# Sorting the neighbour lists of the first two blocks, and starting each layer on them beside the last tails of the layer before

## The chip, the cores and the metric

The kernel runs on one NeuronCore of a Trainium2 chip. The metric is the device time of one execution in microseconds, taken as the median of several runs; less is better. The engines are called PE (TensorE, matmuls), DVE (VectorE), ACT (ScalarE), POOL (GpSimd, which also issues every indirect transfer) and SP (SyncE).

## The reference

Four graph layers run over 2048 nodes, a batch of 8 and 128 features. All use one random adjacency matrix in which an entry is 1 with chance 1/128, so a node has about 16 neighbours. Layers 0 and 1 are attention layers with 8 heads, layers 2 and 3 are graph attention with one score per edge:

```
# layers 0 and 1
Q, K, V = h@Wq, h@Wk, h@Wv                          # 8 heads of 16
attn = softmax(where(adj == 0, -inf, Q.K / 4))       # over the neighbours m of n
x = layernorm(h + attn@V @ Wo + bo)
x = layernorm(x + relu(x@W1 + b1)@W2 + b2)
# layers 2 and 3
h = x@W;  e = leaky_relu(h@a_src [of i] + h@a_dst [of j], 0.2)
out = softmax(where(adj == 0, -inf, e)) @ h
x = layernorm(out + x)
```

## The kernel before, in words

**Places and blocks.** The kernel treats the matrix as sparse. `start()` reads it, lists the neighbours of every node, and counts the nodes by their number of neighbours. `rank` holds the place of each node in falling order of that number, and `perm` holds the nodes by place. The 2048 places are cut into 16 blocks of 128 nodes (t = 0 to 15), one node to a partition. Block t has `CAPS[t]` list slots, 30 for block 0 down to 11 for block 15. The last two slots of block 0 (`FOLD`) are a folded part that holds the further neighbours of the 16 largest nodes. A list that is shorter than its block's slots ends in entries that point outside the table. `find_lists(t)` fills `lists` and the mask `lmask` for one block; it runs beside layer 0.

**Tables.** Layer l reads its neighbours' rows from the DRAM tensor `tables[l]`: one row for each node, of 8 x 256 floats (keys and values, 8 KB) in layers 0 and 1, and of 8 x 130 floats (4160 bytes) in layers 2 and 3. `gather` (L299) is one indirect transfer, issued by POOL, that fetches the rows of one list slot for the 128 nodes of a block. Since neighbours are random, a slot can need any row of the table. `put_rows` (L419) is the indirect transfer that writes a finished block's rows into the table of the next layer.

**Chunks.** A layer's slots are worked off in chunks, of two slots in layers 0 and 1 and of four in layers 2 and 3. A chunk's rows land in one of six buffers (`KVB`), and up to three chunks (four in layers 2 and 3, `AHEAD`) are fetched ahead of the one in work. An attention chunk is a product on DVE (L528), a sum on DVE (L531), exponentials on ACT (L537), a product on DVE (L542) and matmuls with the identity that add the slots up in PSUM (L552). A chunk of layers 2 and 3 is four small DVE operations (L667 to L673), a large product on DVE (L679) with the last two of eight batches on ACT (L684), an addition of halves on DVE (L688), and matmuls (L694).

**Tails.** When a block's last chunk is done, `sums` takes reciprocals of the weights' sums, `outputs` (L565, L571) scales the accumulator, and two tails (`attention_tail` or `gat_tail`, one for each half of the batch) do the projections, the layer norms and the next layer's rows. A norm is squares on ACT (L406), a power on POOL (L411) and a scaling on ACT (L415). When both halves are done, `state_done` stores the block's state to DRAM (`kept`) and calls `put_rows`.

**Order.** The order of every engine's instructions is written by hand. Chunks and tails are Python generators; each `yield` ends a step. The main loop in `layer(l)` makes one trip for each chunk, in which it issues the chunk's own steps and calls `slot()` three times; a `slot()` advances every open tail by one step. At the end of a layer `drain()` runs the open tails to their ends, and only then does the next call of `layer` issue its first gathers. So the three boundaries between layers are places where the last tails run with no chunk beside them: the first gathers of layer l + 1 come after the last `put_rows` of layer l.

**Other names the change touches.** `w` holds a block's weights (one buffer), `val` a row of the matrix in `start()` (two buffers), `qf` the queries for the folded part of block 0, `over` collects the overflow checks that `verdict()` turns into a flag; if it is not zero, a general dense path follows.

Of the kernel before, what the change touches and what calls it, by code (L numbers as in the profile page):

```python
# [8 lines left out]
F32 = mybir.dt.float32  # L9
F16 = mybir.dt.float16  # L10
BF16 = mybir.dt.bfloat16
FP8 = mybir.dt.float8e4
I32 = mybir.dt.int32
# [4 lines left out]
P = 128  # L18
B, N, D = 8, 2048, 128
NT = N // P  # L20
NH = 8
# [7 lines left out]
NB = 8  # L29
CHUNK = 4 * NB * (D + 2)  # L30
KVB = 6
AHEAD = (3, 3, 4, 4)
SCALED = 2


# [1 line left out]

BASE, MANY, FOLD = 28, 16, 2
CAPS = [BASE + FOLD, 23, 21, 20, 19, 18, 18, 17, 16, 16, 15, 14, 14, 13, 12, 11]
SEG = 128  # L40
BINS = 64

# [4 lines left out]
def split(s, n):  # L47

    k = -(-s // n)
    return [s // k + (i < s % k) for i in range(k)]  # L50


def pieces(t, n):

    res, k = [], 0
    for m in split(CAPS[t] if t > 0 else BASE, n):
        res.append((k, m, False))
        k += m
    if t == 0:
        res.insert(1, (BASE, FOLD, True))  # L60
    return res


# [1 line left out]
def sparse_path(ctx: ExitStack, tc: tile.TileContext, ins: dict, out: bass.AP, flag: bass.AP):  # L65
# [60 lines left out]
    def buffer():  # L126
        turn[0] += 1
        return bufs[turn[0] % KVB]
# [4 lines left out]
    lists = const.tile([P, sum(CAPS)], I32, name="lists")  # L133
    lmask = const.tile([P, sum(CAPS)], F32, name="lmask")
    first = [sum(CAPS[:t]) for t in range(NT)]

    own = const.tile([P, NT, B], F32, name="own")
    score = const.tile([P, 2, NT, 2 * B], F32, name="score")
# [142 lines left out]
    def width(l):  # L281
        return NB * (2 * D if l < 2 else D + 2)
# [12 lines left out]
        nc.sync.dma_start(xT.rearrange("p b n -> p (b n)"), kept[t])  # L295
        return xT

    def gather(l, at, dst):
        nc.gpsimd.indirect_dma_start(  # L299
            out=dst, out_offset=None, in_=tables[l][:, :],  # L300
            in_offset=bass.IndirectOffsetOnAxis(ap=lists[:, at : at + 1], axis=0),
            bounds_check=N - (l < 2), oob_is_err=False,
        )

# [23 lines left out]
    def find_lists(t):  # L328
# [45 lines left out]
        )  # L374
        yield

    def folded_sums(w, box):

        columns = w.shape[-1]
        ps = misc()[:, :columns]  # L380
        for i in range(FOLD):
            nc.tensor.matmul(ps, merge, w[:, i, :], start=i == 0, stop=i == FOLD - 1)
        box["folded"] = small.tile([P, columns], F32, tag="folded", name="folded", bufs=1)
        nc.scalar.copy(box["folded"], ps)
# [15 lines left out]
    def normed(z, dst):  # L400

        yield

        ss = small.tile([P, 4], F32, tag="ss", name="ss", bufs=3)
        for i in range(4):
            nc.scalar.activation(  # L406
                dst[:, i, :], z[:, i, :], AF.Square, bias=eps, scale=D**-0.5,
                accum_out=ss[:, i : i + 1],
            )
        rs = small.tile([P, 4], F32, tag="rs", name="rs", bufs=3)  # L410
        nc.gpsimd.tensor_tensor(rs, ss, half, op=ALU.pow)  # L411
        yield
        yield
        for i in range(4):
            nc.scalar.mul(dst[:, i, :], z[:, i, :], rs[:, i : i + 1])  # L415
        yield

    def put_rows(l, t, rows):
        nc.gpsimd.indirect_dma_start(  # L419
# [54 lines left out]
    def state_done(l, t, box):  # L474


        box["halves"] = box.get("halves", 0) + 1
        if box["halves"] == 2:
            if l < 3:
                nc.sync.dma_start(kept[t], box["x"].rearrange("p b n -> p (b n)"))  # L480
                put_rows(l + 1, t, box["rows"])
            box["state"](t + 3)


    def attention_begin(l, t, box):
# [2 lines left out]
            yield  # L488
        xT = box["x"]
        if t == 0:  # L490
            qf = work.tile([P, NB, D], F32, tag="q", name="qf")
        box["q"] = q = work.tile([P, NB, D], F32, tag="q", name="q")
        for i in range(0, NB, 4):
            pq = misc().rearrange("p (b c) -> p b c", c=D)
# [25 lines left out]
    def attention_chunk(l, c):  # L520
        box, t, k, ns = c["box"], c["t"], c["k"], c["ns"]
        if k == 0:
            box["acc"] = pacc.tile([P, NB // 4, 512], F32, tag="acc", name="acc")
            box["w"] = work.tile([P, max(CAPS), NB * NH], F32, tag="w", name="w", bufs=1)
        acc, w, q = box["acc"], box["w"], box["qf" if c["folded"] else "q"]
        kv = c["buf"].rearrange("p s (b c) -> p s b c", b=NB)
        kk = kv[:, :, :, :D]
# [212 lines left out]
    def start():  # L740
# [81 lines left out]
            nc.scalar.activation(junk, src, AF.Relu, bias=onesc, scale=-1.0, accum_out=dst)  # L822

        def neighbours(t):
            val = work.tile([P, N], F16, tag="val", name="val")
            nc.vector.scalar_tensor_tensor(
                val, adj[t % 6], 0.0, iota1, op0=ALU.not_equal, op1=ALU.mult
            )
# [69 lines left out]
        part1 = small.tile([P, NT], F32, tag="part1", name="part1", bufs=1)  # L898
        nc.vector.tensor_copy(part1, pn[:, :NT])
        nc.vector.tensor_add(perm, part1, pn[:, NT : 2 * NT])  # L900

        nc.vector.scalar_tensor_tensor(
            over[:, 0, :], left, float(N - N // SEG * 8), none, op0=ALU.add, op1=ALU.subtract
# [31 lines left out]
    threads = []  # L935
    tails = []

    def advance(group):
        for g in list(group):
            if next(g, 0) == 0:  # L940
                group.remove(g)

    def slot():
        advance(threads)
        advance(tails)

    def drain():
        while threads or tails:
            advance(threads)
            advance(tails)  # L950

    def tail(l, t, box):
        def rest():
            for _ in range(2 if l < 2 else 3):
                yield
            outputs(l, t, box)
            part = attention_tail if l < 2 else gat_tail
            tails.append(part(l, t, box, 0))
            tails.append(later(3, lambda: part(l, t, box, 4)))
            yield  # L960

        tails.append(rest())

    def later(n, make):
        for _ in range(n):
            yield
        yield from make()

    def layer(l):
        boxes = [{} for _ in range(NT)]  # L970
        att = l < 2
        per = 2 if att else 4
        chunks = []
        for t in range(NT):
            for k, ns, folded in pieces(t, per):
                chunks.append(dict(t=t, k=k, ns=ns, folded=folded, box=boxes[t], last=False))
            chunks[-1]["last"] = True
        n = len(chunks)

        def fetch(c):  # L980
            if c >= n:
                return
            c = chunks[c]
            c["buf"] = buffer()[:, : c["ns"] * width(l)].rearrange("p (s c) -> p s c", s=c["ns"])
            for i in range(c["ns"]):
                gather(l, first[c["t"]] + c["k"] + i, c["buf"][:, i])

        def state(t):
            if t < NT:
                if l == 0:  # L990
                    threads.append(fetch_state(t, boxes[t]))
                else:
                    boxes[t].update(x=load_state(t), ready=True)

        for box in boxes:
            box["state"] = state

        def begin(t):
            if att:
                threads.append(attention_begin(l, t, boxes[t]))  # L1000

        if l == 0:
            threads.append(find_lists(0))
            state(0)
            drain()
        for i in range(AHEAD[l]):
            fetch(i)
        if l > 0:
            state(0)
        drain()  # L1010
        begin(0)
        drain()
        if l == 0:
            threads.append(find_lists(1))
        run = [(attention_chunk if att else gat_chunk)(l, c) for c in chunks]

        def go(i, times=1):

            if 0 <= i < n:
                for _ in range(times):  # L1020
                    next(run[i], None)

        def is_last(i):
            return 0 <= i < n and chunks[i]["last"]

        def end(i):
            t = chunks[i]["t"]
            tail(l, t, chunks[i]["box"])

        for i in range(n + 2):  # L1030
            fetch(i + AHEAD[l])
            if i < n and chunks[i]["k"] == 0:
                t = chunks[i]["t"]
                if l == 0 and t + 2 < NT:
                    threads.append(find_lists(t + 2))
                if t == 0:
                    state(1)
                    threads.append(later(12, lambda: state(2) or iter(())))
                while att and "asked" not in chunks[i]["box"]:
                    advance(threads)  # L1040
            if i + 2 < n and chunks[i + 2]["k"] == 0:
                begin(chunks[i + 2]["t"])
            if att:

                go(i - 2)
                if is_last(i - 2):
                    end(i - 2)
                go(i)
                slot()
                go(i)  # L1050
                slot()
                if is_last(i - 1):
                    sums(l, chunks[i - 1]["t"], chunks[i - 1]["box"])
                go(i - 1, 2)
                slot()
            else:


                if i + 1 < n and chunks[i + 1]["folded"]:
                    go(i + 1)  # L1060
                if is_last(i - 1):
                    sums(l, chunks[i - 1]["t"], chunks[i - 1]["box"])
                go(i)
                slot()
                go(i)
                slot()
                go(i - 1, 2)
                if is_last(i - 1):
                    end(i - 1)
                slot()  # L1070
        if l == 3:
            verdict()
        drain()

    with tc.manual_schedule():
        start()
        for l in range(4):
            layer(l)


@with_exitstack
# [522 lines left out]
```

## Time and profile before

| what | value |
|---|---|
| median of 3 runs | 3457.39 us (3457.35 to 3460.24) |
| the profiled execution | 3462.36 us, of which the span is 3460.6 us |
| busy share of the span | PE 79%, PE weight loads 46%, DVE 88%, ACT 41%, POOL 61% |
| mean granted PE clock | 0.916 |
| gathers (L299) | 1108, mean 1465 ns on POOL each |
| writes of rows (L419) | 48, mean 1537 ns on POOL each |
| DMA traffic | 980 MB, 283 GB/s over the span |
| DVE busy in layer 1, 1280 to 2240 us | 952.28 of 960 us |
| DVE busy in layer 2, 2340 to 2840 us | 430.58 of 500 us |

The busy shares are means over four layers and a preparation of some 180 us. The page also cuts the span into 40 slices of 86.5 us and gives each engine's busy share in tenths for each slice; stages with different limits are told apart there.

### The profile page before, as it was taken

What the parts mean: (1) busy time and instruction counts of PE and PEld (TensorE: products, weight loads), DVE (VectorE), ACT (ScalarE), POOL (GpSimd) and SP (SyncE); (2) the same over time, 40 slices, a digit from 0 to 9 for tenths busy, and PEclk for the clock granted to TensorE, in tenths of its full rate; (3) what the DMA queues carried; (4) which work ended last, traced back from release to release, by engine and by line L of the source; (5) the groups of instructions that cost most, each with busy time, mean ns of one, the idle gap of its engine ahead of it and who ended that gap; (6) DMA issues with size and microseconds to landing.
All of it is one profiled execution on the core that took longest, in us unless ns stands there. A gap on an engine that the chain in (4) does not pass through costs nothing. (4 is left out here: it accounts for less than half of the span.)

```text
span 3460.6 us, 34591 instructions
## 1 busy us (share of the span) xinstructions
PE 2749.7 (79%) x10618; PEld 1587.6 (46%) x10618; DVE 3055.0 (88%) x2685; ACT 1435.0 (41%) x4972; POOL 2125.4 (61%) x1441
## 2 busy tenths in 40 slices
PE   5657888799899966888888989975888995668675
PEld 4523455455555542444555556652444552223332
DVE  7789999999999929999999999938888875888886
ACT  5612333344344440233333434443555663444444
POOL 0053666666667533555677766628878756888874
PEclk9878999899999989989999999998999997988888
DMA  8486778888878547777887888729999967989883
GB/s 339 179 306 248 282 280 299 321 294 304 315 295 313 211 167 281 266 295 294 307 299 306 293 305 304 283 69 337 334 327 346 336 266 275 321 301 317 299 292 123
DMA packets 195887, 980.13 MB, mean 283 GB/s; under 512 B 28334, under 2 KB 30128, under 8 KB 124084
## 3 DMA queue, kind: packets, MB, share of 16 engines
q0 software_dynamic: 172352, 884.08, 70.2%
q1 hardware_dynamic: 18438, 75.51, 5.7%
q10 hardware_dynamic: 4904, 18.24, 1.4%
q8 instruction: 87, 1.43, 0.2%
q14 instruction: 106, 0.87, 0.1%
HBM read 937.13 MB, written 85.21 MB: 295 GB/s over the span
## 5 line engine op out<-in xcount | busy, mean ns | idle before, releaser
L299 POOL DMA_INDIRECT kv<-table,lists x1108 | 1622.8, 1465 | 523.7 <-issue 240.9
L552 PE MATMUL acc<-kv,ident 128*128 128x512 f32 x2200 | 1110.6, 636 | 257.7 <-DVE kv L542 257.4
L694 PE MATMUL acc<-kv,ident 128*128 128x512 f32 x1184 | 610.2, 664 | 236.7 <-DVE kv L688 191.1
L552 PEld LDWEIGHTS acc<-kv,ident 128*128 128x128 f32 x2200 | 413.4, 201 | 698.6 <-issue 368.2
L528 DVE TENSOR_TENSOR kv<-kv,q 128x2048 f32<-128x2048 f32 (+1 forms) x282 | 629.3, 2232 | 69.5 <-DMA kv<-table,lists 63.3
L531 DVE TENSOR_REDUCE sc<-kv 128x128 f32<-128x2048 f32 (+1 forms) x284 | 634.1, 2233 | 9.4
L411 POOL TENSOR_TENSOR rs<-ss,half 128x4 f32<-128x4 f32 x192 | 318.2, 1657 | 518.2 <-ACT n L406 517.1
L542 DVE TENSOR_TENSOR kv<-kv,w 128x2048 f32<-128x2048 f32 (+1 forms) x284 | 631.4, 2223 | 0.0
L406 ACT ACTIVATE n<-m,eps 128x128 f32<-128x128 f32 x768 | 271.9, 367 | 544.6 <-PE m L634 216.8
L694 PEld LDWEIGHTS acc<-kv,ident 128*128 128x128 f32 x1184 | 240.1, 213 | 543.3 <-issue 295.8
L679 DVE TENSOR_TENSOR kv<-kv,pair 128x3072 f32<-128x3072 f32 (+1 forms) x150 | 466.2, 3108 | 0.9
L684 ACT ACTIVATE kv<-kv,ws 128x128 f32<-128x128 f32 x1108 | 339.0, 403 | 189.2 <-DVE ws L673 86.8
L688 DVE TENSOR_TENSOR kv<-kv 128x2048 f32<-128x2048 f32 (+1 forms) x150 | 296.0, 1974 | 110.5 <-ACT kv L684 104.9
L537 ACT ACTIVATE w<-sc,lmask 128x64 f32<-128x64 f32 x554 | 164.6, 349 | 521.5 <-DVE sc L531 406.9
L415 ACT ACTIVATE n<-m,rs 128x128 f32<-128x128 f32 x768 | 219.6, 369 | 328.6 <-POOL rs L411 321.9
L406 ACT ACTIVATION_READ_ACCUMULATOR n<-m,eps 128x1 f32 x768 | 157.2, 205 | 0.0
L634 PE MATMUL m<-w_L_w,hT 128*128 128x128 f32 x1024 | 156.3, 275 | 0.0
L308 PE MATMUL m<-ident,n 128*128 128x128 f32 x640 | 105.9, 286 | 46.2 <-ACT n L415 45.7
L419 POOL DMA_INDIRECT table<-rows,perm x48 | 73.8, 1537 | 104.4 <-ACT rows L443 46.0
L634 PEld LDWEIGHTS m<-w_L_w,hT 128*128 128x128 f32 x1024 | 135.0, 192 | 0.0
L613 PE MATMUL m<-n1T,w_L_gnn_W 128*128 128x512 f32 x256 | 131.3, 597 | 3.3 <-ACT n1T L608 3.3
L308 PEld LDWEIGHTS m<-ident,n 128*128 128x128 f32 x640 | 81.6, 146 | 103.4 <-ACT n L415 49.9
(219 smaller groups left out, 3029.5 us busy)
## 6 DMA issues: line engine op xcount, KB each, us to landing
kept<-xT SPq DMA_DIRECT2D x48, 512.0 KB
xT<-kept SPq DMA_DIRECT2D x48, 512.0 KB
kv<-table,lists POOLq DMA_INDIRECT x1108
kv<-in_adj_dram SPq DMA_DIRECT2D x16, 1024.0 KB
table<-kv ACTq DMA_DIRECT2D x16, 1024.0 KB
kv<-in_x_nodes_dram SPq DMA_DIRECT2D x16, 512.0 KB
found<-cand POOLq DMA_DIRECT2D x16, 64.0 KB
table<-rows,perm POOLq DMA_INDIRECT x48
```

What stands on the lines that cost most here:

```text
L299: nc.gpsimd.indirect_dma_start(out=dst, out_offset=None, in_=tables[l][:, :], in_offset=bass.IndirectOffsetOnAxis(ap=lists[:, at : at + 1] ...
L406: nc.scalar.activation(dst[:, i, :], z[:, i, :], AF.Square, bias=eps, scale=D**-0.5, accum_out=ss[:, i : i + 1],)
L411: nc.gpsimd.tensor_tensor(rs, ss, half, op=ALU.pow)
L528: nc.vector.tensor_mul(kk, kk, q[:, None].to_broadcast([P, ns, NB, D]))
L531: nc.vector.tensor_reduce(sc[:, :ns].rearrange("p s (b h) -> p (s b) h", h=NH), kk.rearrange("p s b (h j) -> p (s b) h j", h=NH), axis=AX. ...
L542: nc.vector.tensor_mul(vv, vv, w[:, k : k + ns, :].rearrange("p s (b h) -> p (s b) h", h=NH)[:, :, None, :] .to_broadcast([P, ns * NB, HD, ...
L552: nc.tensor.matmul(acc[:, j, :], merge if c["folded"] else ident, kv[:, i, 4 * j : 4 * j + 4, D:], start=k + i == 0, stop=c["last"] and i ...
L634: nc.tensor.matmul(y[:, j, :], hT[:, f, j, :], wt["2"][:, f, :], start=False, stop=f == 1, skip_group_check=True,)
L679: nc.vector.tensor_mul(hv[:, :, :nv, :], hv[:, :, :nv, :], wc[:, :, :nv, None].to_broadcast([P, ns, nv, D]))
L684: nc.scalar.mul(hv[:, i, b, :], hv[:, i, b, :], ws[:, i, b - nv : b - nv + 1])
L688: nc.vector.tensor_add(hv[:, : ns - left], hv[:, : ns - left], hv[:, left:ns])
L694: nc.tensor.matmul(acc[:, j, :], merge if c["folded"] else ident, hv[:, i, 4 * j : 4 * j + 4, :], start=k + i == 0, stop=c["last"] and i = ...
```

## The change

`order_lists(t)`, new, runs beside layer 0 for blocks 0 and 1 (from blocks 2 and 6 on). It fetches the place of every neighbour, one indirect transfer of 128 numbers per slot, from a new DRAM tensor `ranks`, and sorts the list by place with rounds of the 8-fold maximum. It also adds to `over` that the slots named in `EARLY` lie in the blocks named there: of block 0 the first 8 slots must not need the last 3 blocks, the first 12 not the last 2, the first 16 not the last one; of block 1 the first 8 not the last 3 and the first 12 not the last one.

The four layers become one list `every` of chunks and one loop. In layers 1 to 3 the first 28 slots (16 of block 0 and 12 of block 1, in the order of `ORDER`) come first, then the rest of block 0 with its folded part, the rest of block 1, and the other blocks as before. `fetch()` issues a chunk's gathers as soon as a buffer may be taken and `put[l]`, the number of blocks written to the layer's table, has reached what the chunk needs. There is no `drain()` between layers; where the loop reaches a chunk that is not fetched yet, it calls `slot()` until it is.

`clear_late()`, new, writes zeros to the rows of the last three blocks in the tables of layers 1 to 3, beside the first blocks of layer 0. `w` gets a second buffer and shares it with `val`, and in layer 1 `qf` moves to another buffer.

```diff
-AHEAD = (3, 3, 4, 4)
+EARLY = (((8, 3), (12, 2), (16, 1)), ((8, 3), (12, 1)))
+ORDER = {2: ((0, 0, 12), (1, 0, 8), (0, 12, 16), (1, 8, 12)),
+         4: ((0, 0, 8), (1, 0, 8), (0, 8, 16), (1, 8, 12))}
...
+    def order_lists(t):
+        n = (BASE, CAPS[1])[t]
+        mine = lists[:, first[t] : first[t] + n]
+        place = small.tile([P, BASE], F32, tag="place", name="place", bufs=1)
+        nc.vector.memset(place, float(N))
+        for k in range(n):
+            nc.gpsimd.indirect_dma_start(
+                out=place[:, k : k + 1], out_offset=None, in_=ranks[:, :],
+                in_offset=bass.IndirectOffsetOnAxis(ap=mine[:, k : k + 1], axis=0),
+                bounds_check=N - 1, oob_is_err=False,
+            )
+            for _ in range(3):
+                yield
+        for _ in range(6):
+            yield
+        key = small.tile([P, 32], F32, tag="key", name="key", bufs=1)
+        nc.vector.memset(key, 0.0)
+        nc.vector.scalar_tensor_tensor(
+            key[:, :n], place[:, :n], -4096.0, mine, op0=ALU.mult, op1=ALU.subtract
+        )
+        nc.vector.tensor_scalar_add(key[:, :n], key[:, :n], float(4097 * N))
+        top = small.tile([P, 48], F32, tag="top", name="top")
+        for r in range(0, n, 8):
+            nc.vector.max(top[:, r : r + 8], key)
+            if r + 8 < n:
+                nc.vector.match_replace(key, top[:, r : r + 8], key, 0.0)
+        yield
+        for i, b in EARLY[t]:
...
+        to = sorted_lists[:, t * BASE : t * BASE + n]
...
+    def clear_late():
+        rows = rows_of(blocks[0][0])
+        nc.vector.memset(rows, 0.0)
+        for l in (1, 2, 3):
+            for t in range(NT - 3, NT):
+                for _ in range(3):
+                    yield
+                put_rows(l, t, rows)
...
                 put_rows(l + 1, t, box["rows"])
-            box["state"](t + 3)
+                put[l + 1] += 1
+            state(l, t + 3)
...
-            box["w"] = work.tile([P, max(CAPS), NB * NH], F32, tag="w", name="w", bufs=1)
+            box["w"] = work.tile([P, max(CAPS), NB * NH], F32, tag="w", name="w")
...
+        nc.sync.dma_start(ranks.rearrange("(t p) o -> p (t o)", p=P), rank)
...
+    def fetch():
+        while now[1] < len(every):
+            c = every[now[1]]
+            l, t, k, ns = c["l"], c["t"], c["k"], c["ns"]
+            if now[1] - now[0] > (4 if now[1] >= KVB and every[now[1] - KVB]["l"] > 1 else 3):
+                return
+            resorted = l > 0 and t < 2 and not c["folded"]
+            need = NT - max([b for end, b in EARLY[t] if k + ns <= end] + [0] if resorted else [0])
+            if put[l] < need:
+                return
+            c["buf"] = buffer()[:, : ns * width(l)].rearrange("p (s c) -> p s c", s=ns)
...
+            now[1] += 1
     def slot():
         advance(threads)
         advance(tails)
+        fetch()
...
+        tails.append(later(1, lambda: part(l, t, box, 0)))
+        tails.append(later(4, lambda: part(l, t, box, 4)))
...
+        for i in range(len(every) + 2):
+            now[0] = i
+            fetch()
+            c2, c1, c, n1, n2 = (chunk(i + j) for j in range(-2, 3))
...
+                    if t == 0:
+                        state(0, 1)
+                        threads.append(later(12, lambda: state(0, 2) or iter(())))
+                        threads.append(later(12, clear_late))
+                    if t in (2, 6):
+                        threads.append(order_lists(t // 4))
...
+            while i < len(every) and now[1] <= i:
+                slot()
```

## The prediction

> **What bounds the kernel now.** I read the slices of the span first. DVE stands at 9 tenths or more through layer 0, layer 1 and most of layer 2, with three holes, and the DMA row has a hole just before or in each:
>
> ```profile
> DVE  7789999999999929999999999938888875888886
> DMA  8486778888878547777887888729999967989883
> ```
>
> The holes are the three boundaries between layers. DVE is the bound elsewhere: the table by stages gives it 952.28 of 960 us in layer 1 and 430.58 of 500 us in layer 2. Next I took the waits of DVE over the whole span (who waited for whom, total us, times, longest):
>
> ```profile
> DVE kv L688 <- ACT kv L684: 104.9, 44, 6.3
> DVE kv L667 <- DMA kv<-table,lists: 98.8, 15, 53.6
> DVE kv L528 <- DMA kv<-table,lists: 63.3, 2, 53.1
> ```
>
> Nearly all waiting for gathers is one wait per boundary; within the layers transfers are in time. The timeline of DVE shows both halves of each hole (start, duration, in brackets the idle time before):
>
> ```profile
> 1226.06 1.23 DVE L565 TENSOR_TENSOR o<-acc,sums 128x1024 f32<-128x1024 f32 x1 [8.27 <-PE acc L552]
> 1280.38 2.29 DVE L528 TENSOR_TENSOR kv<-kv,q 128x2048 f32<-128x2048 f32 x1 [53.10 <-DMA kv<-table,lists]
> ...
> 2285.24 1.23 DVE L565 TENSOR_TENSOR o<-acc,sums 128x1024 f32<-128x1024 f32 x1 [8.14 <-PE acc L552]
> 2340.06 0.19 DVE L667 TENSOR_TENSOR kv<-kv,own 128x32 f32<-128x32 f32 x1 [53.59 <-DMA kv<-table,lists]
> ...
> 2850.88 1.23 DVE L571 TENSOR_TENSOR o<-acc,sums 128x1024 f32<-128x1024 f32 x1 [9.07 <-PE acc L694]
> 2889.15 0.19 DVE L667 TENSOR_TENSOR kv<-kv,own 128x32 f32<-128x32 f32 x1 [37.05 <-DMA kv<-table,lists]
> ```
>
> DVE stands idle for 61.4, 61.7 and 46.1 us, 169 us in all: what the change can win at most. The timeline of POOL tells what the gathers wait for:
>
> ```profile
> 1240.37 1.04 POOL L419 DMA_INDIRECT table<-rows,perm  x1 [0.18 <-issue]
> ...
> 1263.33 1.03 POOL L419 DMA_INDIRECT table<-rows,perm  x1 [5.87 <-ACT rows L443]
> 1271.44 1.04 POOL L299 DMA_INDIRECT kv<-table,lists  x1 [7.08 <-DMA table<-rows,perm]
> ```
>
> These are the writes of blocks 14 and 15. Counted from the end of DVE's work (1217.8), they come after 23 and 45 us, the first gather 8.1 us after the last write, the first rows on DVE 9 us later. At the second boundary it is 23, 45, 7.8 and 10 us, at the third 19, 32, 5.3 and 10 us.
>
> **What the Trainium skill says.** "DMA: Bandwidth & Descriptors", section "Two DMAs through the same engine are not ordered": only the semaphore tells that data has landed, so the issuer waits. The trace agrees: POOL stood 7.08 us. Section "Anatomy of one DMA — SWDGE (gpsimd) path": a transfer takes about 2.0 us plus bytes/436e3; for a write of 1.05 MB that is 4.4 us (estimate), for 0.53 MB 3.2 us. The trace has 8.1 and 5.3 to 7.8 us from issue to the next gather; I use those.
>
> **The change, part by part.**
>
> *Order of issue.* A trip is one chunk and has three slots. A tail half of layer 0 yields 20 times, the second half starts 4 slots after `outputs`, so block 15's write comes 24 slots after `outputs` (trip 1 of the new layer): in trip 9. Its rows are first needed by chunk 14, fetched in trip 11: no stop. Into layer 2, chunks hold four slots and only 7 are early; 23 slots after trip 1 is past trip 7, so the loop runs out of fetched chunks and spins some 8 slots. In layer 3 the tail is short (12 slots), the write comes at the end of trip 5.
>
> *Boundary 0 to 1.* 14 early chunks at 6.85 us (three rows of 2.285) are 96 us of DVE work over a hole of 61.4. PE was busy 42.75 of the 51 us after 1217; with 14 chunks at 4 x 0.636 us that makes 78 of 96 us, so it fits. New is a wait in both directions on POOL: a write must wait for the early gathers of the same table that were issued before it, and the next gathers wait for the write. Behind these stand, on the same engine, the powers (L411) of block 15's tail, and behind those ACT's scaling and the next exponentials. Timeline from the start of trip 0: gathers of chunk 6 issued at 26 us, landed at 34; write of block 14 at 34 instead of 31, landed at 42; chunk 7's gathers issued at 42 and landed at 51, wanted at 49. I take 2 us for each of the writes of blocks 13, 14 and 15. Gain 61.4 - 6 = 55 us; bounds 35 (each turn stops DVE for 9 us, a landing) and 61.
>
> *Boundary 1 to 2.* A chunk is 6.2 us of DVE (0.55 + 3.35 + 2.29): 7 chunks, 43.4 us, less than the hole. The fetch of chunks 5 and 6 needs block 14. Its write comes at 29 us, lands at 36, eight gathers take POOL until 47, chunk 5's rows are there at 46 where trip 5 began at 34. The powers of block 15's second half wait on POOL until 47. From there before needed 19 us to the last write; with chunks 5 and 6 in ACT's and PE's queues between, and 8 spun slots at 39/28 = 1.4 us, I get a write at 68 instead of 49 (45 plus 3.5 of trip 0), 8 us to its landing and 9 to the rows: DVE goes on at about 84.5 instead of 66.5. Gain 43.4 - 18 = 25 us; bounds 5 and 43.
>
> *Boundary 2 to 3.* Block 14's write is issued at 22 us, lands at 28; chunk 5's rows are there at 39 instead of the wanted 33, chunk 6 ends at 51. Block 15's write is issued at 45, lands at 50.5, chunk 7's rows come at 59 instead of 49.5. Gain 43.4 - 9.5 = 34 us; bounds 15 and 43.
>
> *Sorting.* DVE is the bound of layer 0, so its work counts in full. Nearest rows: MAX8 on 128 numbers 0.29 us, match-replace with its load 0.37, small operations 0.15 to 0.2. `order_lists(0)`: 4 and 3 of the first two (2.3 us as an upper bound at that width; 1.5 taken at 32), 13 small ones 2.0: 3.5 us; block 1: 2.4 us. The zeroed 128 x 2048 tile: memsets of 64 and 192 words take 0.112 and 0.218 us, 0.83 ns a word, so 1.8 us. Sum 7.7 us. VectorE: DVE Perf Modes, section "Zero memsets can be issued as uint32 (trn2)", gives one cycle per element, about the same.
>
> *Transfers of the sorting and clearing.* 51 fetches of places, each like L331 (1.38 us on POOL), one per trip: 70 us on a POOL that was busy 577.5 of 910 us in layer 0. A chunk's gathers are issued some 20 us ahead and need 11 (3 issue, 8 landing), so 9 us of cover hide them; without cover each costs 1.4 us. The nine writes of zeros are 3 x 1.05 + 6 x 0.53 = 6.3 MB between about 220 and 280 us, where the DMA share was 0.89, 0.65 and 0.58: the free 17.6 us at 370 GB/s carry 6.5 MB. I take 3 us, bounds 0 and 17. The store of `rank` as 2048 single numbers on SP's queue runs beside the first gathers, on which DVE waited 10.2 us at 178 us: no row shows its like; bounds 0 and 8, taken 3.
>
> *No cost.* The second `w`, the move of `qf` and `val` leave every instruction as it was; the exponentials' wait on the single `w` (ACT idle) was not on DVE's path. The tails start within one slot of where they did.
>
> *Sum.* 55 + 25 + 34 - 7.7 - 3 - 3 = 100. The profiled execution took 3462.4 us (span 3460.6 and 1.8 around it), so 3362; the median of the runs was 5 us lower, so **3357 us**, 2.9% less.
>
> **Rivals.**
>
> *The turns between write and gather eat the gain* (0.20). Each boundary has three such turns. If POOL's order costs a full landing of write and of gather each time (16 us of DVE idle) and the tails slip likewise, the boundaries give 20, 5 and 15: 40 - 14 = 26 us, about 3430; a milder form lies anywhere between 3385 and 3445. For it: POOL issues in order and ACT waits on its powers (L415, 321.9 us in the table of waits). Against: 20 us of lead.
>
> *All holes but the shortfalls of chunks close* (0.10). Tails run on at their old pace: 61 + 43.4 - 1 + 43.4 - 1 = 146, less 10: about 3320 down to 3305. Against it: the chain of block 15 interleaves with chunks on ACT and PE.
>
> *Slower: the fetches of places clog layer 0* (0.09). Each is 128 packets of 4 bytes in the one software queue ahead of rows that DVE needs. The skill ("Measured (HBM→SBUF, 128 partitions, SWDGE, issued from GpSimd)") has 0.68 us for 4 KB, which is harmless; no run here shows it. But if each held back the rows by more than its cover, the point from which it decides is (114 - 14)/51 = 2 us of lost DVE time per fetch; at 4 us layer 0 grows by 204 us and the whole to about 3560. Against: the fetches of `found` (L331) stopped DVE just 3.3 us, once.
>
> *The check fails and the dense path follows* (0.01). Worked out from the reference's adjacency: the latest place among the first 8, 12 and 16 sorted neighbours of block 0 is 1265, 1516 and 1788, with limits 1664, 1792 and 1920; for block 1 1176 and 1594, limits 1664 and 1920. So it should not.
>
> **How the numbers follow.** The forecast has 0.60 and spans 3315 to 3395 by its bounds. 8 in 10 is reached with the milder part of the first rival on one side and most of the second on the other: 3308 to 3430. About 0.2%, 7 us, is what a measurement of this kernel can tell from no change. Faster: 0.60 + 0.10 + 0.19 of the first rival = 0.89; slower: 0.09 + 0.01 = 0.10; same 0.01.
>
> **What would show it.** The slices of DVE: the first hole gone, the other two shrunk to some 20 and 10 us, where DVE waits for gathers (L667's line number moved) of chunks that need block 15. The first wait on rows in layers 2 and 3 should come at chunk 5, before the write of block 15. On POOL, gathers of the next layer stand between the writes of blocks 13, 14 and 15, and the writes wait on gathers. Layer 0 is longer by some 10 us. A layer 0 that grows by over 40 us would show the prediction wrong, as would a first boundary with a DVE wait of over 20 us.

## The result, and the profile after

| | median, us | against before, same chip |
|---|---|---|
| before | 3458.81 (3457.35 to 3464.69) | |
| after | 3419.34 (3418.65 to 3421.15) | 0.9884 [0.9866, 0.9901] |

The kernel is 39.5 us faster, 1.2%. The forecast was 100 us. The sign is as forecast and the time lies inside the range of 3308 to 3430; the size is 40% of the forecast.

The slices of the span after, read like those of before:

```profile
DVE  7789999999999989999999999965888876788885
DMA  8487877888888777687887887757999986789883
```

The first hole is gone (the 2 at the fifteenth digit has become an 8). The second one, a 3 before, has become a 6 and a 5; the third, a 7 and a 5, is now a 7 and a 6, and the slice behind it has fallen from 8 to 7. DMA's 4 and 2 in the first two holes are now a 7 and a 5. The waits of DVE over the whole span (who waited for whom, total us, times, longest):

```profile
DVE kv L766 <- ACT kv L762: 147.3, 52, 10.0
DVE kv L745 <- DMA kv<-table,lists: 46.0, 2, 33.5
DVE kv L745 <- DMA kv<-table,sorted_lists: 26.9, 9, 11.1
...
DVE kv L606 <- DMA kv<-table,lists: 10.1, 1, 10.1
...
DVE kv L606 <- DMA kv<-table,sorted_lists: 6.4, 2, 5.1
```

Waiting for gathers fell from 162.1 us (98.8 and 63.3) to 89.4 (the sum of the four lines with DMA), but waiting for ACT in layers 2 and 3 rose from 104.9 to 147.3, and its longest wait from 6.3 to 10.0 us. So a part of the hole turned into another wait. The timeline of DVE shows where (start, duration, in brackets the idle time before):

```profile
1276.20 2.29 DVE L620 TENSOR_TENSOR kv<-kv,w 128x2048 f32<-128x2048 f32 x1 [5.47 <-ACT w L615]
...
1326.29 2.31 DVE L606 TENSOR_TENSOR kv<-kv,q 128x2048 f32<-128x2048 f32 x1 [5.07 <-DMA kv<-table,sorted_lists]
...
2290.26 0.19 DVE L745 TENSOR_TENSOR kv<-kv,own 128x32 f32<-128x32 f32 x1 [11.11 <-DMA kv<-table,sorted_lists]
2335.77 0.18 DVE L745 TENSOR_TENSOR kv<-kv,mine 128x16 f32<-128x16 f32 x1 [33.49 <-DMA kv<-table,lists]
...
2826.28 2.29 DVE L766 TENSOR_TENSOR kv<-kv 128x2048 f32<-128x2048 f32 x1 [9.02 <-ACT kv L762]
2852.55 0.21 DVE L745 TENSOR_TENSOR kv<-kv,own 128x32 f32<-128x32 f32 x1 [10.04 <-DMA kv<-table,sorted_lists]
2877.89 0.17 DVE L745 TENSOR_TENSOR kv<-kv,mine 128x16 f32<-128x16 f32 x1 [12.53 <-DMA kv<-table,lists]
```

The first boundary has no wait over 5.5 us. The second has two, 11.1 us at chunk 5 (the first that needs block 14) and 33.5 us at the first that needs block 15. The third has a wait for ACT ahead of these two kinds. How that wait for ACT comes about is seen on POOL and ACT at the third boundary. POOL first:

```profile
2812.54 1.05 POOL L494 DMA_INDIRECT table<-rows,perm  x1 [5.95 <-DMA kv<-table,sorted_lists]
2816.74 1.03 POOL L320 DMA_INDIRECT kv<-table,sorted_lists  x1 [3.15 <-DMA table<-rows,perm]
...
2820.69 1.00 POOL L320 DMA_INDIRECT kv<-table,sorted_lists  x1 [0.30 <-issue]
2821.71 1.05 POOL L476 TENSOR_TENSOR rs<-ss,half 128x4 f32<-128x4 f32 x1
...
2836.87 1.05 POOL L494 DMA_INDIRECT table<-rows,perm  x1 [0.18 <-issue]
2841.07 2.33 POOL L320 DMA_INDIRECT kv<-table,sorted_lists  x1 [3.15 <-DMA table<-rows,perm]
...
2851.49 0.99 POOL L320 DMA_INDIRECT kv<-table,sorted_lists  x1 [0.30 <-issue]
2852.49 1.05 POOL L476 TENSOR_TENSOR rs<-ss,half 128x4 f32<-128x4 f32 x1
2863.33 2.96 POOL L494 DMA_INDIRECT table<-rows,perm  x1 [9.79 <-ACT score L547]
2870.28 1.03 POOL L320 DMA_INDIRECT kv<-table,lists  x1 [3.99 <-PE acc L772]
```

The three L494 are the writes of blocks 13, 14 and 15. The first waits 5.95 us for early gathers of the same table, the next gathers wait for its landing, and behind them stands a power (L476) of a tail. The same happens after the write of block 14: gathers from 2841.07 on, and the power of block 15's tail only at 2852.49. Now ACT:

```profile
2822.80 1.14 ACT L480 ACTIVATE n<-m,rs 128x128 f32<-128x128 f32 x4 [10.84 <-POOL rs L476]
2823.81 2.44 ACT L762 ACTIVATE kv<-kv,ws 128x128 f32<-128x128 f32 x8
...
2853.58 1.14 ACT L480 ACTIVATE n<-m,rs 128x128 f32<-128x128 f32 x4 [11.52 <-POOL rs L476]
2854.59 2.45 ACT L762 ACTIVATE kv<-kv,ws 128x128 f32<-128x128 f32 x8
...
2956.88 0.37 ACT L471 ACTIVATE n<-m,eps 128x128 f32<-128x128 f32 x1 [10.97 <-DMA out_dram<-n,perm]
2972.34 0.37 ACT L471 ACTIVATE n<-m,eps 128x128 f32<-128x128 f32 x1 [9.85 <-DMA out_dram<-n,perm]
```

ACT stands 10.84 and 11.52 us for those powers, and its share of an early chunk (L762) stands behind the scaling; DVE's 9.02 us follow from the first of the two; the second holds up block 15's tail. The last two lines lie in the slice behind the third boundary that fell from 8 to 7: squares of a tail wait for an output store to leave one of the two buffers of `n`.

**Accounts by block.** I took the time at which DVE starts each block's `outputs` (L643, L649; before L565, L571) and subtracted the time of before. The differences of these landmarks show where the time was won and lost in the profiled executions (3421.15 less 3462.36, -41.2 us). Each is one execution: the first line runs from +5.8 to +13.7 us over the eleven versions that leave this stretch as it is here, or change only the buffers of `n` in it, so steps of a few us say little.

| stretch | change, us |
|---|---|
| up to block 13 of layer 0 | +10.9 |
| boundary 0 to 1 (block 13 to block 2) | -49.9 |
| rest of layer 1 | +0.2 |
| boundary 1 to 2 | -7.7 |
| rest of layer 2 | -2.9 |
| boundary 2 to 3, up to block 1 of layer 3 | -8.1 |
| from block 1 to block 2 of layer 3 | +14.9 |
| rest of layer 3 | +4.8 |
| after the last `outputs` | -3.4 |

### The profile page after: what moved, and what is told of

It is laid out like the page before. It is cut to its first block, busy times and chain, and to the rows that moved or that the text cites. A ratio compares the mean times of both kernels' runs of the same rounds, so it can differ in the third digit from the quotient of the medians.

```text
span 3419.3 us, 34694 instructions
## 1 busy us (share of the span) xinstructions
PE 2746.3 (80%) x10618; PEld 1585.2 (46%) x10618; DVE 3063.5 (90%) x2727; ACT 1429.0 (42%) x4972; POOL 2213.2 (65%) x1501
## 4 chain that ended last, share of the span: by engine, by line
DVE 34%; PE 23%; issue 18%; DMA 10%; POOL 6%; ACT 3%; POOLq 0%; DVEq 0%; ACTq 0%
DVE kv L620 12%; DVE kv L606 12%; PE acc L630 7%; PE acc L772 6%; DMA kv<-table,lists 5%; POOL kv L320 4%; DVE sc L609 2%; DVE kv L757 2%; DMA kv<-table,sorted_lists 2%; DVE kv L766 2%; PE m L712 2%; DVE sums L455 1%; DMA table<-rows,perm 1%; PE m L329 1%; PE m L691 1%
## 5 line engine op out<-in xcount | busy, mean ns | idle before, releaser
L320 POOL DMA_INDIRECT kv<-table,lists x955 | 1422.8, 1490 | 352.6 <-issue 205.8
L606 DVE TENSOR_TENSOR kv<-kv,q 128x2048 f32<-128x2048 f32 (+1 forms) x282 | 629.4, 2232 | 18.9 <-DMA kv<-table,lists 10.1
L476 POOL TENSOR_TENSOR rs<-ss,half 128x4 f32<-128x4 f32 x192 | 290.5, 1513 | 422.6 <-ACT n L471 421.1
L766 DVE TENSOR_TENSOR kv<-kv 128x2048 f32<-128x2048 f32 (+1 forms) x150 | 296.2, 1975 | 147.3 <-ACT kv L762 147.3
L762 ACT ACTIVATE kv<-kv,ws 128x128 f32<-128x128 f32 x1108 | 339.4, 406 | 146.3 <-DVE ws L751 118.9
L320 POOL DMA_INDIRECT kv<-table,sorted_lists x153 | 199.9, 1307 | 114.5 <-PE acc L630 47.6
L494 POOL DMA_INDIRECT table<-rows,perm x57 | 106.5, 1868 | 110.2 <-ACT rows L518 26.4
L329 PEld LDWEIGHTS m<-ident,n 128*128 128x128 f32 x640 | 81.5, 146 | 142.2 <-ACT n L480 92.7
```

What stands on the lines that cost most here:

```text
L320: nc.gpsimd.indirect_dma_start(out=dst, out_offset=None, in_=tables[l][:, :], in_offset=bass.IndirectOffsetOnAxis(ap=index, axis=0), bound ...
L606: nc.vector.tensor_mul(kk, kk, q[:, None].to_broadcast([P, ns, NB, D]))
L762: nc.scalar.mul(hv[:, i, b, :], hv[:, i, b, :], ws[:, i, b - nv : b - nv + 1])
L766: nc.vector.tensor_add(hv[:, : ns - left], hv[:, : ns - left], hv[:, left:ns])
```

## The experiments

**Which parts pay.** The first two runs keep the sorting, the clearing and the common loop. One starts only layer 1 early, the other no layer (two empty trips stand there between the layers).

```diff
-        for t, k, end in ORDER[n]:
+        for t, k, end in ORDER[n] if l == 1 else ():   # second run: if l > 4
...
-            need = NT - max([...] if resorted else [0])
+            need = NT - max([...] if resorted and l == 1 else [0])   # second run: and l > 4
```

> Only layer 1 starts with the 28 early slots; layers 2 and 3 start in plain order after the last write of the layer before, as in the kernel before. Read from the blocks' times in the two traces, the first boundary gained 50 us, the second 8 (and 3 more within layer 2), the third lost 7. If that reading is right, taking the early slots out of layers 2 and 3 costs about 4 us: 3423 us (3415 to 3432). If the prediction's gains of 25 and 34 us were there and something else had eaten them, this kernel would stand near 3478.

Measured: 3420.69 us, 0.9887 [0.9870, 0.9903], the time of the whole change. What the early slots of layers 2 and 3 save, those layers give back. Without early chunks beside them the last tails of layers 1 and 2 take just as long as before (from a write of block 13 or 12 to that of block 15, 56.4 and 54.4 us in both kernels), so it isn't the new loop that changes them.

> Sorting, clearing and the common loop stay, but no layer starts on early slots. This prices the sorting and clearing alone: by the blocks' times of layer 0 it is 11 us on top of the kernel before, so 3470 us (3464 to 3476). If the common loop itself had changed the layers (tails moved by a slot, second buffer of weights), it would show as a difference beyond that.

Measured: 3470.24 us, 1.0026 [1.0015, 1.0037], 8.9 us slower than before. This is the price of the change: sorting, clearing, the place fetches and the new loop together.

**The turn at block 14.** Here all early slots need blocks 0 to 12 only, so no early gather has to wait for the write of block 14. This graph allows it for 14 slots of block 0 and 12 of block 1, two fewer than the change has. The order changes with it: all early slots of block 0 now come before those of block 1.

```diff
-EARLY = (((8, 3), (12, 2), (16, 1)), ((8, 3), (12, 1)))
-ORDER = {2: ((0, 0, 12), (1, 0, 8), (0, 12, 16), (1, 8, 12)),
-         4: ((0, 0, 8), (1, 0, 8), (0, 8, 16), (1, 8, 12))}
+EARLY = (((14, 3),), ((12, 3),))
+ORDER = {n: ((0, 0, 14), (1, 0, 12)) for n in (2, 4)}
```

> The early slots are 14 of block 0 and 12 of block 1, all of which need only the first 13 blocks, so no early chunk waits for blocks 14 or 15 by its need; but all gathers still read the one table that the late blocks are written to, so writes and gathers go on waiting for each other. Theory of the turns (the waits between writes and gathers of one table on POOL, with the tails' powers queued behind them, hold the tails up): the turns remain wherever a write stands between two early chunks, so the gain is small, 3400 to 3415 us. Theory of the pace (the tails are late because their steps alternate with chunks' steps on ACT and PE): no change but for the chunks that no longer wait for block 14, some 10 us at each of two boundaries, 3395 to 3420. This run does not tell the two apart; it is the control of the next.

Measured: 3389.84 us, 0.9793 [0.9777, 0.9810], 29.5 us faster than the change and better than I expected. POOL at the third boundary in this run:

```profile
2801.84 1.05 POOL L493 DMA_INDIRECT table<-rows,perm  x1 [3.04 <-DMA kv<-table,sorted_lists]
2806.05 1.03 POOL L319 DMA_INDIRECT kv<-table,sorted_lists  x1 [3.15 <-DMA table<-rows,perm]
...
2831.49 1.05 POOL L493 DMA_INDIRECT table<-rows,perm  x1 [5.86 <-DMA kv<-table,sorted_lists]
2832.57 1.04 POOL L475 TENSOR_TENSOR rs<-ss,half 128x4 f32<-128x4 f32 x1
2841.55 1.03 POOL L493 DMA_INDIRECT table<-rows,perm  x1 [7.94 <-ACT score L546]
```

After the write of block 14 (2831.49) the power follows at once, and the write of block 15 comes 10.1 us later; in the change it was 26.5, before 12.7. At the second boundary the same distance is 30.4 us here, 46.6 in the change and 21.8 before.

**A second table.** As above, and blocks 0 to 12 also write a copy of the table, from which the early gathers read. Then no early gather waits for a late write, and no late write for an early gather.

```diff
+    early = [dram.tile([N + (l > 1), width(l)], F32, name=f"early{l}") for l in range(1, 4)]
...
                 put_rows(l + 1, t, box["rows"])
+                if t < NT - 3:
+                    put_rows(l + 1, t, box["rows"], early[l])
...
-                gather(l, index, c["buf"][:, i])
+                gather(l, index, c["buf"][:, i], early[l - 1] if need < NT else None)
```

> As the run with 14 and 12 early slots, but these slots are gathered from a second copy of the table that only blocks 0 to 12 (and zeros for the rest) are written to. The writes of blocks 13 to 15 go to the first table alone, so no early gather waits for them and they wait for no early gather. Cost: 39 more writes of rows (25 MB), hidden in layers 0 and 1, up to 20 us in layer 2. Theory of the turns: the two late boundaries give what the prediction had or more, 3340 to 3375 us. Theory of the pace: the tails stay as late as with one table, and the run is within 10 us of that one, or slower by the writes.

Measured: 3410.46 us, 0.9850 [0.9833, 0.9866]. The 39 further writes cost 15 us each in layers 0 and 2 (26.7 us by block 13 of layer 0 where the kernel with one need has 12.0). The boundaries gain 8, 0 and 4 us more than there. So once block 14 is out of the early slots, the waits between the writes of blocks 13 to 15 and the early gathers are a small part of what is still missing at the second and third boundary.

**The buffers of the norm.** The give-back of 14.9 us between blocks 1 and 2 of layer 3 was still 14.2 with one need. The early slots make blocks 0 and 1 end three to four chunks apart, so that their four tail halves meet. Three runs give `n` a third buffer: with one need, in the kernel before, and in the change.

```diff
-        n1 = work.tile([P, 4, D], F32, tag="n", name="n1")
+        n1 = work.tile([P, 4, D], F32, tag="n", name="n1", bufs=3)
...
-        n2 = work.tile([P, 4, D], F32, tag="n", name="n2")
+        n2 = work.tile([P, 4, D], F32, tag="n", name="n2", bufs=3)
```

> The run with 14 and 12 early slots in one table, with a third buffer for the normed rows (n1, n2). In layer 3 blocks 0 and 1 now end close together, and ACT waits 20 us for the stores of the output that still read both buffers. Theory of the give-back: this is part of what the third boundary lost, 8 to 12 us come back, 3378 to 3382 us. Rival: it is idle time of ACT that no DVE wait hangs on; within 3 us of 3390.

Measured: 3368.27 us, 0.9734 [0.9717, 0.9751], 21.6 us less than with one need alone, and the fastest version of all.

> The kernel before with a third buffer for the normed rows, nothing else. Control for the give-back: in layer 3 of the kernel with the change, ACT waits 21 us for output stores around the ends of blocks 0 and 1, which lie 3 chunks apart. If that collision comes from the early slots, the third buffer does little for the kernel before (within 5 us, or up to 8 faster for the short blocks at the end of layer 3). If it is as good here as with the change, 12 us or more, it is no part of the change's account.

Measured: 3455.12 us, 0.9985 [0.9977, 0.9994]; the kernel before gains 4.3 us from the buffer.

> The change as it is, with a third buffer for the normed rows. Theory of the give-back: the step of 15 us that layer 3 loses between the ends of its blocks 1 and 2 shrinks to some 3, so 3400 to 3408 us. Rival (the gain in the run with one need came from the start of the kernel and the end of layer 3): within 8 us of 3419.

Measured: 3397.05 us, 0.9823 [0.9807, 0.9840]; the change gains 22 us. The step from block 1 to block 2 of layer 3 falls from 14.9 to 2.9 us, which is 12 of them. Another 7 us come in the rest of layer 3, where the kernel before gains 6.6 from the buffer too. The waits of ACT from 2878 to 2994 us in the change begin with

```profile
ACT n L471 <- DMA out_dram<-n,perm: 20.8, 2, 11.0
```

and this wait is missing with the third buffer. The loss between these two blocks is a collision that the change made and a buffer takes away.

**ACT's share and the pace of the tails.** With one need the last write still came 24 to 27 us late at each of these two boundaries. Two guesses: ACT's two batches of each early chunk hold up the tails; or the tails advance too rarely, three steps to a chunk. The first kernel gives early chunks of layers 2 and 3 all eight batches on DVE, the second advances the tails twice per slot while an early chunk is in work, the third has both and the buffer.

```diff
+        nv = NB if c["early"] else NB - SCALED
...
         advance(tails)
+        if now[0] < len(every) and every[now[0]]["early"]:
+            advance(tails)
```

> The same base; the early chunks of layers 2 and 3 do all eight batches of the large product on DVE (3 of 4 before), so DVE's next step in them waits for no work of ACT. It costs 1.1 us of DVE per early chunk, 7 to 8 us per boundary, 15 in all. Theory that ACT is the link (ACT stands in its queue at a tail's scaling that waits for POOL's power, and the chunk's scaled batches stand behind it): the waits of DVE on ACT in early chunks (about 15 us at the second boundary, 20 at the third) go, but the tails are no faster and the wait for the last write takes most of it back at the second boundary; net -5 to -15 us at the third, 3375 to 3395 in all. Rival, that the tails' own length sets the end: the end of each boundary stays where it was, 3390 to 3400.

Measured: 3389.04 us, 0.9793 [0.9777, 0.9810]; nothing gained over one need. DVE's waits for ACT's share fall by 16.2 us (from 139.1 to 122.9), but those for rows rise by 8.6 and DVE has the two batches to do.

> The same base; while an early chunk of layers 2 and 3 is in work, every slot advances the open tails by two steps. Theory of the pace (the tails are late because one step per slot is issued between chunks): block 15's write comes up to 6 slots' worth earlier, the wait of 33 us before the first slot that needs it shrinks by 8 to 15 us at the second boundary, 3370 to 3385 us. Theory of the turns and of the queue on ACT (the steps wait for powers and for chunks, not for their place in the program): no gain or a loss, 3387 to 3400.

Measured: 3411.34 us, 0.9856 [0.9839, 0.9872]; 21.5 us slower. The waits of DVE, first with one need, then with the double step:

```profile
DVE kv L765 <- ACT kv L761: 139.1, 48, 9.2
DVE kv L744 <- DMA kv<-table,lists: 41.5, 2, 32.7
```

```profile
DVE kv L765 <- ACT kv L761: 187.7, 55, 18.5
...
DVE kv L744 <- DMA kv<-table,lists: 13.1, 3, 11.4
```

The waits for rows fall by 28 us, those for ACT rise by 49. A faster pace of issue isn't what was missing. (That the tails' steps now stand on ACT ahead of the chunks' and aren't ready yet is my reading of it, not shown apart.)

> The three edits together. If pace, ACT and the output stores each held a part, they add up: 3355 to 3370 us. If the length of the tail's chain sets the end, it stays within 10 us of 3390.

Measured: 3386.61 us, 0.9784 [0.9768, 0.9801]; with the buffer alone it was 3368, so the two other edits cost 18 us here and the parts don't add up. (Run singly, only the double step cost time.)

**Powers away from POOL.** In two kernels the tails of blocks 13 to 15 take 1.5 - 0.5 s on DVE in place of the power on POOL, which leaves the true norm out.

```diff
-        nc.gpsimd.tensor_tensor(rs, ss, half, op=ALU.pow)
-        yield
+        if late:
+            yield
+            nc.vector.tensor_scalar(rs, ss, -0.5, 1.5, op0=ALU.mult, op1=ALU.add)
+        else:
+            nc.gpsimd.tensor_tensor(rs, ss, half, op=ALU.pow)
+            yield
```

> The run with 14 and 12 early slots and the third buffer, where the tails of blocks 13 to 15 (in layer 3 none) take their powers no longer on POOL: a line 1.5 - 0.5 s stands for the power, computed on DVE one slot later (it leaves the true norm out). It costs DVE 30 small operations, some 5 us. Theory of the turns (powers queued on POOL behind gathers and writes that wait): these tails get shorter, the waits of ACT on POOL and the 33 us at the second boundary shrink; 3340 to 3358 us. Rival (the length of the chain itself and ACT's and PE's work beside chunks): within 6 us of 3368, or slower by the work on DVE.

Measured: 3409.50 us, 0.9857 [0.9841, 0.9874]; 41 us slower than the same kernel with powers on POOL.

> The same edit of the powers and the third buffer on the change itself, with its 28 early slots and the need for block 14 in the middle. Theory that the turn at block 14 costs by the powers queued behind its gathers: most of the 26 us that the run with one need won at the two late boundaries comes here too, 3375 to 3390 us. Theory that it costs by the late rows of chunks 5 and 6 themselves: these wait as before, 3395 to 3408.

Measured: 3413.17 us, 0.9871 [0.9855, 0.9888]; 16 us slower than the change with the third buffer. The waits of DVE in the first of the two say why:

```profile
...
DVE rs L477 <- ACT n L470: 90.4, 29, 8.4
DVE kv L748 <- DMA kv<-table,lists: 34.5, 3, 20.2
```

DVE now waits 90.4 us in its own queue for ACT's squares, more than was to be won. Against the same kernel with powers on POOL its waits for ACT's share fall by 39.1 us (from 131.8 to 92.7) and those for unsorted rows by 10.0 (from 44.5), which leaves the 41 us. The third boundary did improve, by 6.7 us up to block 1 in the second kernel (17.4 against 10.7), the first two got worse by 14.6 and 13 us. The experiment put a new wait in the place of the old one, so it doesn't settle how much of the rest the powers hold.

## Why the prediction was right and wrong

**Right:** the sign, the first boundary and the cost in layer 0. Boundary 0 to 1 gave 49.9 us where the sum had 55. Layer 0 cost 10.9 us in the profiled execution (8.9 in the run without early slots, by its median) where it had 13.7: 3.3 at its start, then 3.8 and 3.4 at blocks 4 and 8, where the two sortings fall (7.2 for an expected 5.9). The 3.3 are no evidence for the 3 us of the stored `rank`: with the same start they are anything from -1.1 to 6.2 in the other runs. The rival in which place fetches clog layer 0 is out: the fetches took 87.0 us of POOL (51 at 1.7 us), and DVE's one wait for unsorted rows in layers 0 and 1, the 10.1 us shown above, is that at the start of layer 0, which before has too. The places of chunk 5, of block 15 and of the gathers between the writes are as foretold.

**Wrong: the slip of the last write.** For boundaries 1 to 2 and 2 to 3 the prediction took 43.4 us of early work less the time by which block 15's write and rows come later: 18 and 9.5 us. That form of the sum is good, its second term is not: it measured 39.1 us at both. The three writes of the second boundary, before and after:

```profile
2265.79 1.05 POOL L419 DMA_INDIRECT table<-rows,perm  x1 [0.21 <-issue]
...
2300.35 1.04 POOL L419 DMA_INDIRECT table<-rows,perm  x1 [0.18 <-issue]
...
2322.17 1.03 POOL L419 DMA_INDIRECT table<-rows,perm  x1 [5.22 <-ACT mine L657]
```

```profile
2226.97 1.05 POOL L494 DMA_INDIRECT table<-rows,perm  x1 [0.21 <-issue]
...
2275.84 1.06 POOL L494 DMA_INDIRECT table<-rows,perm  x1 [0.18 <-issue]
...
2322.47 1.06 POOL L494 DMA_INDIRECT table<-rows,perm  x1 [5.22 <-ACT rows L545]
```

The table gives the time to block 15's write, for 1 to 2 from block 13's write, for 2 to 3 from block 12's (there block 13's already slips), and the slip, which is that time less the one of before:

| | 1 to 2: time, slip | gain | 2 to 3: time, slip | gain up to block 1 |
|---|---|---|---|---|
| before | 56.4 | | 54.4 | |
| forecast | 18 | 25 | 9.5 | 34 |
| change | 95.5, 39.1 | 7.7 | 93.5, 39.1 | 8.1 |
| one need | 83.3, 26.9 | 18.5 | 78.7, 24.3 | 23.4 |
| two tables | 81.3, 24.9 | 18.7 | 74.3, 19.9 | 27.6 |
| one need, double step | 87.7, 31.3 | 13.8 | 86.5, 32.1 | 13.5 |

43.4 less 39.1 is 4.3, and 7.7 and 8.1 were measured (8.1 lies below the prediction's lower bound of 15); in every row of a run, slip and gain add up to 44 to 48 us. Beside early chunks the last tails took almost as much longer as the chunks' work is worth.

**Which steps of its timeline failed.** Counted in us from the start of trip 0 (in the trace, the first operation of the first early chunk on DVE: 2234.88 and 2799.70), the prediction against the trace:

| | 1 to 2: forecast, trace | 2 to 3: forecast, trace |
|---|---|---|
| write of block 14 | 29, 41.0 | 22, 37.2 |
| chunk 5's rows on DVE | 46, 55.4 | 39, 52.9 |
| write of block 15 | 68, 87.6 | 45, 63.6 |
| rows that need block 15 on DVE | 84.5, 100.9 | 59, 78.2 |

So 12 of the 19.6 us by which block 15's write misses the forecast at the second boundary, and 15 of 18.6 at the third, are there already when block 14 is written, before its turn begins. The turn at block 14, which the prediction did price, was too low by 8 and 3 us; what it put at next to nothing was the delay of the tails before it (29 us for block 14's write where the old pace is 26.5, and 22 where it is 22.5). At the third boundary it overlooked a turn at block 12, whose write the very first early gathers wait for. On POOL, before and after:

```profile
2819.23 2.88 POOL L419 DMA_INDIRECT table<-rows,perm  x1 [0.30 <-issue]
2822.88 1.04 POOL L411 TENSOR_TENSOR rs<-ss,half 128x4 f32<-128x4 f32 x1 [0.77 <-ACT n L406]
```

```profile
2769.81 2.88 POOL L494 DMA_INDIRECT table<-rows,perm  x1 [0.30 <-issue]
2779.48 1.03 POOL L320 DMA_INDIRECT kv<-table,sorted_lists  x1 [6.79 <-DVE ws L751]
...
2784.44 1.04 POOL L476 TENSOR_TENSOR rs<-ss,half 128x4 f32<-128x4 f32 x1
```

Before, the power comes 3.7 us after the write of block 12; with the change it stands behind four early gathers and comes after 14.7. ACT then waits 12.21 us for it (before 1.23) and DVE 6.82 us for ACT (before 1.9 at most), all while layer 2 is still at work. (The view puts the end of the 6.79 us down to an operation of DVE; with one need the same wait, of 6.97 us, is put down to the landing of the write.) At the next turn block 13's write slips by 17.5 us (landmark of block 13 -49.4, its write -31.9).

**Where the slip comes from.** Taking the early slots that need block 14 away removes 12 and 15 us of it: it falls to 26.9 and 24.3. (That run has two slots fewer and another order too; two slots are some 3 us of DVE, an estimate from 6.2 us for four.) The chain in the profile is the one shown with the result, from the write over eight gathers and the power to ACT and back to the tail. The first rival, in its milder form, is a part of what took place at the second and third boundary. At the first the last write slips too, by 36.7 us (1310.88 against 1263.33 us, less the 10.9 by which block 13 is later), but against 96 us of early work, of which the hole could use 61.4.

**Wrong: nothing was counted for layer 3 behind the boundary.** The prediction ended a boundary where DVE goes on. But blocks 0 and 1, whose slots are interleaved, end close together; their tails met on two buffers of `n`, and 14.9 us were lost. The third buffer shows this cause: 2.9 us are left. One need and the third buffer together bring the kernel to 92.8 us below the one before, of which some 4 us are the buffer's gain without the change.

**Open.** Some 24 to 27 us of slip per boundary remain with one need, 18.4 of 26.9 at the second boundary and all of it at the third before block 14 is written. ACT's share and the pace of issue don't account for it; the powers couldn't be told apart from what replaced them. The turn at block 12 of the third boundary stands in these runs too (ACT waits 12.39 us for the power with one need, 12.62 with two tables, where the early gathers wait for block 12's write to the second table), so the run with two tables rules out the later turns there, not this one. What the slip would be without it no run shows. One rival no run tests is PE. The prediction asked only at the first boundary whether the chunks' matmuls fit beside the tails'. Between the writes of blocks 13 and 15 at the second boundary PE is busy 49.4 of 56.4 us before, 74.8 of 83.3 with one need and 76.3 of 95.5 with the change; the chunks' matmuls into `acc` are 11.3, 34.6 and 37.7 us of that. With one need PE's busy time in that stretch grew by 25.3 us where the slip is 26.9. At the third boundary (from block 12's write) it grew by 11.9 us, from 50.4 to 62.2, where the slip is 24.3, so PE alone would not explain that one. The mean granted clock of PE in these stretches at the second boundary was 1.00 before, 0.92 with one need and 0.89 with the change; whether that is a cause of the waits or follows from them no run shows. That the tails are late because PE was nearly full is a reading of these numbers, not shown by an experiment.

## What to carry to other kernels

Work that is moved beside a tail is worth its own time less the time by which it makes the tail end later; estimate that delay for each tail that runs beside it, not the last alone, and from every queue the two share: one where a transfer's wait stands ahead of small operations that another engine needs, and an engine that the tail alone already fills. Early work should ask only for what is finished well ahead: here two slots fewer, with one need in place of three, brought 29.5 us. And a new order changes which blocks end together, so the buffers of their tails must be counted anew.

## What the runs showed of the hardware

- From the issue of a 0.53 MB write to that of the gather that waits for it took 4.2 us at the writes of blocks 13 and 14 of the third boundary (2812.54 to 2816.74, 2836.87 to 2841.07) and 6.0 us at block 15's write of the second (2322.47 to 2328.42). At block 12's write, with gathers of layer 2 still under way, it took 9.9 us in the run with one need (2762.88 to 2772.73). The Trainium skill, "DMA: Bandwidth & Descriptors", section "Anatomy of one DMA — SWDGE (gpsimd) path", gives 3.2 us (estimate) for the transfer, so the trace has 1 to 7 us more. The prediction had taken 5.3 to 8 us for the writes of blocks 14 and 15, so for these it was not the term that failed.
- A fetch of 128 single numbers took POOL 1.7 us on average (87.0 us for 51), about as long as a gather of 128 rows of 8 or 4 KB (1.5 us). In layers 0 and 1 DVE had just one wait for unsorted rows, and it stood at the start of layer 0.
